# A graph layer on one core: ScalarE's copies ahead of its squares, a tail in another order, and an opening with gamma as a row

## The chip, the cores and the metric

The kernel runs on one core of a Trainium2 chip. The metric is the device time of one execution in microseconds (us), and less is better. The engines have instruction queues of their own: TensorE (PE in the profile, its weight loads PEld), VectorE (DVE), ScalarE (ACT), GpSimd (POOL) and SyncE (SP). An engine works through its queue in order; SP, ACT and POOL also start DMA transfers from theirs.

## The reference

A message-passing layer over 100,000 edges and 6,250 nodes of 128 features, then a residual sum and a layer norm:

```
msg_in = concatenate([x[src], x[dst], edge_attr])     # 100000 x 384
h   = msg_in @ W + b                                  # 100000 x 128
h   = (h - mean(h)) * rsqrt(var(h) + 1e-5) * gamma + beta
msg = relu(h)
out = segment_sum(msg, src, 6250)
return layernorm(x + out)                             # 6250 x 128
```

The edges come sorted by `dst`; `src` is in no order. All inputs are fp32 or int32.

## The kernel before, in words

*Folding.* W has three slices of 128 rows, for `x[src]`, `x[dst]` and the edge's own features. `weights` subtracts each row's mean and multiplies by the sign of gamma (`sgn`, from `signs`), so that the product has mean zero and only the sum of its squares is needed. `project` multiplies x by the first slice into an SBUF table `xa` (three bf16 parts that add up) and by the second into DRAM tables `xb_d`. TensorE does it in the first part of the run.

*Edges.* They lie in 782 tiles of 128, four tiles to a piece: 196 pieces, `q` in the code. For each piece

- SP loads the features (`eT`), the window of `xb_d` that holds the piece's destinations (`win`), and `db`, the destination's place in that window, spread over all partitions from a DRAM copy, `drel_d`. The pieces with `q < BY_PE` have no `db` load: TensorE spreads their row of `drel0` into PSUM with a product against ones. Piece 2's load is issued by POOL, all others by SP (L551).
- `edge_hot` (L577, VectorE) compares `db` with the partition number and so gives a one-hot `ohd`;
- `edges` (TensorE) adds the products `eT` x w (L589) and `ohd` x `win` (L593) in a PSUM tile `hp`;
- `evict` (ScalarE) copies `hp` (L601) and the source's number (L602) to one of eight buffers `hs`;
- `scatters` (L619, POOL) writes each tile with one indirect DMA to `sorted_d[s]`, at rows `place_i`: a bucket sort by source block. From piece 12 to 194 each scatter also waits for a named product of TensorE, so that it is spread over its piece.

`places` computes `place_i` on VectorE, for a group of tiles at a time, from the source numbers that `source_blocks` prepares. `first_windows` and `windows` cast the window places on ScalarE for the first pieces and for all. `clear` has SP fill the ends of the buckets from `empty`, a tile that `clean` fills by POOL's memsets.

*Pairs.* The edges are cut in six splits (`SPLITS`). When a split is sorted, its 50 source blocks are worked off in 25 pairs. A pair takes: a load of the sorted rows `hl`; `ones` (VectorE, a one-hot `ohe`, L691); `turn` (TensorE, its transposition, L703) and `turned` (ScalarE, a copy to `ohn`, L707); `seed` (ScalarE copies `hl` to a PSUM tile `sel`, L713); `pick` (TensorE adds the source's part of h from `xa`, L730); `square` (ScalarE, squares with their sums and the root, L739 and L742); `root` and `scale` (VectorE, L748 and L754: the reciprocal, and the scaled message with its cut at zero); `sums` (TensorE, L763) and `add` (VectorE, L771: into the table `acc`). A pair's tiles are in groups of at most four: two groups in the first four splits, a single one in the fifth.

`FLOW` is a list of these steps with an offset each; `work(n)` goes n steps forward and issues at each step what is due of the pairs under way, in the order of the list. A pair begins every four steps. `steps_due(q)` spreads the steps over the pieces; the fifth split's pairs stand in the last pieces, 1.56 pairs to a piece.

*Tail.* The sixth split's pairs are done in 14 `Unit`s behind the last scatter: one pair, eleven times two, one, one. A unit does what a pair does (load L792, `ones` L799, `turned` L812, `pick` L818 and L824, `square` L835 and L838, `scale` L850, `sums` L864, `add` L870) and then finishes its nodes: `begin` (POOL: `acc` times gamma's size, plus x, L882 and L883), `stats` (VectorE: plus beta's part, with row sums, L888), `var` (ScalarE: squares of the centred rows into `fsq`, their sums, and the root, L898 and L901), `norm` (VectorE, L907 and L909), `end` (POOL, two operations, L915 and L916; for the last unit ScalarE, L919) and the store to `out` (SP, L922). `tail(i)` writes down the order of step i, in which up to five units are at different places.

The order on TensorE, VectorE, ScalarE and SP is the order in which the program is written (`manual_schedule`); POOL's is left to the scheduler. Behind everything a flag is read on all engines (L1184), and a second, general path runs if it isn't zero (L1186); here it is zero.

Of the kernel before, what the change touches and what calls it, by code (L numbers as in the profile page):

```python
# [27 lines left out]
PT = 4  # L28
# [17 lines left out]
BY_PE = 2  # L46
# [37 lines left out]
def fast_path(ctx, tc, io, bad_d):  # L84
# [63 lines left out]
    nc.scalar.dma_start(gamma_bc, dram_ap(io["gamma"], 0, [[0, P], [1, D]]))  # L148
    nc.sync.dma_start(src_i[:, :n0], io["srcT"][:, :n0])
    nc.scalar.dma_start(w3[:, 1, :], w_in[:, 1, :])  # L150
    load_x(0, 1)
    nc.scalar.dma_start(dst0_i, io["dstC"][0:1, 0:BY_PE, :])
    nc.scalar.dma_start(base_i, io["base"])
    nc.scalar.dma_start(w3[:, 2, :], w_in[:, 2, :])
    nc.sync.dma_start(dst_i, io["dstC"])
# [3 lines left out]
    edge_feats(0)  # L159
# [6 lines left out]
    def late_loads():  # L166
        nc.scalar.dma_start(w3[:, 0, :], w_in[:, 0, :])
        for t, v in ((b_bc, io["b"]), (beta_bc, io["beta"])):
            nc.scalar.dma_start(t, dram_ap(v, 0, [[0, P], [1, D]]))
# [50 lines left out]

    def clean():
        for i in range(RUN):
            nc.gpsimd.memset(empty[:, i, 0:D], 0.0)
            nc.gpsimd.memset(empty[:, i, D:ROW], 0.0)
            nc.gpsimd.memset(empty[:, i, D:D + 1], 200.0)
# [17 lines left out]

    def signs():
        nc.vector.tensor_scalar(sgn, gamma_bc, 0.0, 2.0, op0=ALU.is_ge, op1=ALU.mult)
        nc.vector.tensor_scalar(sgn, sgn, -1.0, None, op0=ALU.add)
# [20 lines left out]
    def source_blocks(t0, t1):  # L267
        c = slice(t0, t1)
        nc.vector.tensor_copy(src_f[:, c], src_i[:, c])
# [5 lines left out]
        nc.vector.tensor_copy(bkt_h[:, c], bkt[:, c])  # L275

        nc.vector.tensor_scalar(src_f[:, c], bkt[:, c], 0.5, -0.25, op0=ALU.mult, op1=ALU.add)
        nc.vector.tensor_scalar(src_f[:, c], src_f[:, c], MAGIC, None, op0=ALU.add)
        nc.vector.tensor_scalar(src_f[:, c], src_f[:, c], -MAGIC, None, op0=ALU.add)
# [24 lines left out]
    def first_windows():  # L304
        nc.scalar.mul(minus00, dst0_i[:, :, 0], -1.0)
        for h in range(BY_PE):
            nc.scalar.activation(drel0[:, h, :], dst0_i[:, h, :], AF.Identity,
                                 bias=minus00[:, h:h + 1])
# [217 lines left out]

    def all_checks():
# [10 lines left out]
    clean()  # L538

    def edge_loads(q):  # L540
# [8 lines left out]
        if q >= BY_PE:  # L549
            c1 = g * PT * P  # L550
            (nc.sync if q > 2 else nc.gpsimd).dma_start(  # L551
# [228 lines left out]
    class Unit:  # L780
# [112 lines left out]
        def var(self):  # L893
            fin = late["fin"]
            fsq = fin.tile([P, D], F32, name="fsq", bufs=2)
            var = fin.tile([P, FN], F32, name="var", bufs=2)
            for j in range(self.m):
                nc.scalar.activation(fsq, self.y[:, j, :], AF.Square, scale=-float(D),  # L898
# [45 lines left out]

    constants()
    signs()
    weights(1, 2)
# [3 lines left out]
    first_windows()  # L951
    source_blocks(0, n0)
    run(groups[0])
    run(first)
    run(groups[0])
    bases([0])
    run(groups[0])
    run(first)
    run(groups[0], 2)
    windows()  # L960
    edge_loads(0)
    edge_loads(2)
    edge_window(0)
# [4 lines left out]
    weights(2, 3)  # L968
    run(first)
# [36 lines left out]
    others[at_slots[-1] + 4] = beta_row  # L1006

# [105 lines left out]
    def tail(i):  # L1113
# [51 lines left out]
    units[1].turn()  # L1165
    units[0].square()
    work(4)
# [10 lines left out]
def gnn_resnorm_kernel(ctx, tc, io):  # L1178
# [3 lines left out]
    with ExitStack() as inner:  # L1182
        fast_path(inner, tc, io, bad_t)
    flag = nc.values_load(bad_t[0:1, 0:1], min_val=0, max_val=1 << 20,  # L1184
                          skip_runtime_bounds_check_because="a sum of small counts")
    with tc.If(flag > 0):  # L1186
# [235 lines left out]
```

## Time and profile before

| | |
|---|---|
| time, median of three executions | 1142.15 us (1140.5 to 1145.27) |
| the profiled execution's own time | 1144.18 us |
| its span | 1142.4 us |
| TensorE | 77% busy, 8873 products |
| VectorE | 74%, 2352 instructions |
| ScalarE | 67%, 3115 instructions |
| POOL | 72%, 877 instructions, 782 of them scatters |
| HBM | 215 GB/s over the span |

The profile is a page with the busy time of each engine, the span in forty slices, the DMA queues, the chain of work that ended last, and the groups of instructions. A row of a group names line, engine, operation, output and inputs by the program's names, with the count; then the busy time, the mean of one in ns, the idle time ahead of them, and what ended most of it. Rows in order of time begin with the start and the duration in us, and end in brackets with the wait ahead of them and what ended it. Rows by stretch give the length, and then for an engine its busy time and count; in those for all engines the order is TensorE, its weight loads, VectorE, ScalarE, POOL, and then TensorE's granted clock, the DMA share and GB/s. Rows of waits give the engine, the tile, the line, the releaser, the sum, the count and the longest or mean wait in us.

### The profile page before, as it was taken

To read this page: it belongs to the slowest core of one execution; us is meant where nothing else is said; L and a number is where in the kernel's file an instruction comes from. 1 tells how busy PE (TensorE), PEld (TensorE's weight loads), DVE (VectorE), ACT (ScalarE), POOL (GpSimd) and SP (SyncE) were. 2 spreads that over 40 slices of the span, in tenths; PEclk is the share of its full clock that TensorE was granted. 3 is DMA by queue.
4 is the path that set the end of the run, shared out by engine and by line. 5 is a ranking of instruction groups with operands and counts; after the bars stand their busy time and mean duration, and the time that the engine had idled before them with its cause. 6 is when DMAs were issued, how large, how long until landed. Compare 5 with 4: busy or idle time off the path is not lost.

```text
span 1142.4 us, 27577 instructions
## 1 busy us (share of the span) xinstructions
PE 874.6 (77%) x8873; PEld 811.4 (71%) x8873; DVE 841.6 (74%) x2352; ACT 768.3 (67%) x3115; POOL 817.1 (72%) x877
## 2 busy tenths in 40 slices
PE   3668676537887869787787879888888998777993
PEld 2657565437787868787787869888887888775762
DVE  6875666236877777676868678987989887666984
ACT  3324432207676867677676778988889998776993
POOL 3677777777777777777777777777777776761675
PEclk9688887667988989899899989999999999999996
DMA  7698998457877763887786758776878676744531
GB/s 216 208 274 255 293 290 250 133 175 230 254 255 231 241 202 124 281 244 237 226 262 208 228 185 283 250 228 211 254 225 259 202 236 183 209 127 139 166 131 59
DMA packets 123539, 247.48 MB, mean 217 GB/s; under 512 B 47036, under 2 KB 55245, under 8 KB 123384
## 3 DMA queue, kind: packets, MB, share of 16 engines
q1 hardware_dynamic: 97332, 191.92, 55.0%
q0 software_dynamic: 25184, 53.31, 13.2%
q8 instruction: 71, 1.16, 0.4%
q14 instruction: 84, 0.69, 0.2%
q10 hardware_dynamic: 868, 0.40, 0.2%
HBM read 155.74 MB, written 89.80 MB: 215 GB/s over the span
## 4 chain that ended last, share of the span: by engine, by line
PE 31%; DVE 22%; DMA 22%; ACT 13%; issue 6%; POOL 4%; SPq 1%; ACTq 0%; POOLq 0%; DVEq 0%
DMA sorted<-hs,place_i 16%; PE pa L763 7%; PE sel L730 7%; PE hp L589 7%; DVE msg L754 5%; DMA db<-drel_d 4%; ACT sq L739 3%; DVE sc L437 3%; PE beside L484 3%; ACT sel L713 3%; DVE ohe L691 3%; ACT ohn L707 2%; POOL sorted L619 2%; ACT hs L601 2%; PE hp L593 2%
## 5 line engine op out<-in xcount | busy, mean ns | idle before, releaser
L619 POOL DMA_INDIRECT sorted<-hs,place_i x782 | 757.8, 969 | 253.6 <-issue 102.7
L730 PE MATMUL sel<-xa,ohn 128*128 128x128 bf16 x2550 | 188.1, 225 | 126.5 <-ACT sel L713 125.5
L730 PEld LDWEIGHTS <-ohn 128*128 128x128 bf16 x2550 | 165.4, 101 | 141.4 <-issue 111.4
L589 PE MATMUL hp<-w,eT 128*128 128x128 f32 x1564 | 241.5, 303 | 26.4 <-ACT hs L601 26.4
L739 ACT ACTIVATE sq<-sel 128x128 f32<-128x128 f32 x850 | 224.2, 281 | 47.4 <-PE sel L730 47.4
L589 PEld LDWEIGHTS hp<-w,eT 128*128 128x128 f32 x1564 | 218.8, 214 | 52.3 <-ACT hs L601 28.9
L754 DVE SCALAR_TENSOR_TENSOR msg<-sel,rstd,cut 128x128 f32<-128x128 f32 x850 | 240.7, 345 | 7.9
L601 ACT COPY hs<-hp 128x512 f32<-128x512 f32 x196 | 114.1, 582 | 195.3 <-DMA sorted<-hs,place_i 152.5
L763 PE MATMUL pa<-msg,ohe 128*128 128x130 f32 x1700 | 234.0, 291 | 3.5 <-DVE msg L754 3.0
L763 PEld LDWEIGHTS pa<-msg,ohe 128*128 128x128 f32 x1700 | 214.8, 203 | 5.3 <-DVE msg L754 4.3
L739 ACT ACTIVATION_READ_ACCUMULATOR sq<-sel 128x1 f32 x850 | 179.8, 212 | 0.0
L691 DVE TENSOR_TENSOR ohe<-hl,beside 128x1024 f32<-128x1024 f32 (+2 forms) x125 | 131.6, 1053 | 36.2 <-DMA hl<-sorted 24.5
L713 ACT COPY sel<-hl 128x512 f32<-128x512 f32 (+1 forms) x225 | 127.9, 568 | 14.4 <-DVE msg L754 14.1
L577 DVE TENSOR_SCALAR ohd<-db,part_w 128x512 bf16<-128x512 bf16 x194 | 72.1, 372 | 66.1 <-DMA db<-drel_d 41.3
L707 ACT COPY ohn<-tr 128x1024 bf16<-128x1024 bf16 (+2 forms) x125 | 108.7, 870 | 0.0
L748 DVE RECIPROCAL rstd<-std 128x4 f32<-128x4 f32 (+1 forms) x225 | 38.7, 172 | 91.1 <-ACT std L742 88.1
L593 PE MATMUL hp<-win,ohd 126*128 126x128 bf16 x782 | 82.9, 232 | 2.4 <-DMA win<-xb_d 2.4
L703 PE MATMUL tr<-ident_h,ohe 128*128 128x128 bf16 x850 | 70.4, 224 | 8.7 <-issue 7.4
L742 ACT ACTIVATE std<-ss,eps 128x4 f32<-128x4 f32 (+1 forms) x225 | 66.9, 297 | 7.3
L593 PEld LDWEIGHTS <-ohd 126*128 126x128 bf16 x782 | 66.7, 105 | 6.3 <-issue 2.6
L771 DVE TENSOR_TENSOR acc<-acc,pa 128x260 f32<-128x260 f32 x100 | 41.7, 417 | 29.4 <-PE pa L763 26.6
L703 PEld LDWEIGHTS <-ohe 128*128 128x128 bf16 x850 | 54.6, 100 | 9.4 <-issue 7.6
(193 smaller groups left out, 1038.6 us busy)
## 6 DMA issues: line engine op xcount, KB each, us to landing
eT<-in_eT SPq DMA_DIRECT2D x96, 512.0 KB
hl<-sorted SPq DMA_DIRECT2D x75, 528.0 KB
db<-drel_d SPq DMA_DIRECT2D x96, 256.0 KB
sorted<-empty SPq DMA_DIRECT2D x100, 198.0 KB
hl<-sorted SPq DMA_DIRECT2D x50, 264.0 KB
sorted<-hs,place_i POOLq DMA_INDIRECT x782
hl<-sorted SPq DMA_DIRECT2D x25, 396.0 KB
sorted<-empty SPq DMA_DIRECT2D x50, 132.0 KB
```

The source lines that it names most:

```text
L589: pe(nc.tensor.matmul(hp[:, j, :], eT[:, at], w[:, 2, :], start=j == 0, stop=False, skip_group_check=True), 4)
L593: pe(nc.tensor.matmul(hp[:, j, :], oh[:3 * WN, at], win[:3 * WN, :], start=False, stop=j == m - 1, skip_group_check=True))
L601: nc.scalar.copy(hs[:, :m, 0:D], hp[:, :m, :])
L619: i = nc.gpsimd.indirect_dma_start(out=sorted_d[s][:, :], out_offset=bass.IndirectOffsetOnAxis(ap=place_i[:parts, t:t + 1], axis=0), in_=h ...
L691: nc.vector.tensor_tensor(self.ohe[:, :k, :], self.hl[:, :k, D:D + 1].to_broadcast([P, k, P]), row_bc(iota_p, k), op=ALU.is_equal)
L703: pe(nc.tensor.transpose(tr[:, j, :], half[:, j0 + j, 1::2], ident_h))
L707: nc.scalar.copy(self.ohn[:, :self.k, :], self.tr[:, :self.k, :])
L713: nc.scalar.copy(self.sel[g][:, :m, :], self.hl[:, j0:j0 + m, 0:D])
L730: pe(nc.tensor.matmul(sel[:, j, :], self.ohn[:, j0 + j, :], xa[:, b, i * D:(i + 1) * D], start=False, stop=j == m - 1 and i == 2, skip_gro ...
L739: nc.scalar.activation(sq[:, j, :], self.sel[g][:, j, :], AF.Square, accum_out=ss[:, j:j + 1])
L754: nc.vector.scalar_tensor_tensor(self.msg[:, j0 + j, 0:D], self.sel[g][:, j, :], rstd[:, j:j + 1], cut, op0=ALU.mult, op1=ALU.max)
L763: pe(nc.tensor.matmul(self.pa[:, h, :], self.ohe[:, j, :], self.msg[:, j, :], start=(j == h), stop=(j == k - 2 + h)), 4)
```

## The change

There are four parts.

1. *The opening.* `BY_PE` goes from 2 to 4, so the first four pieces have no `db` load, and the load for piece 4 and all later ones is issued by SP. Gamma comes first as one row; VectorE makes its sign there, TensorE spreads it over the partitions with a product against ones, and ScalarE copies it to `sgn`. The broadcast load of gamma goes to the late loads. The opening's DMAs have another order. `clean` is done by ScalarE, with two copies from a small tile `none`. `source_blocks` and `first_windows` are in two halves, and ten products `warm_up` stand in TensorE's queue.
2. *Copies ahead of squares.* For pairs of a single group, `FLOW` issues `turned` and `seed` at offset 3 and `pick` at offset 5, in list order ahead of the square at 7; pairs of two groups keep their offsets.
3. *The tail.* `begin` of unit i-1 is issued ahead of `end` of unit i-3; `end` of the last two units is done by ScalarE, and `begin` of the last two by VectorE (before: the last one each). The squares in `var` go to slices of a `sq` tile in place of the two buffers `fsq`. The steps between the last pairs and the first units are interleaved in another order.
4. *The flag* is read in the middle of the run, right behind the step that computes it, and no longer at the end.

```
-BY_PE = 2
+BY_PE = 4
...
-    nc.scalar.dma_start(gamma_bc, dram_ap(io["gamma"], 0, [[0, P], [1, D]]))
-    nc.sync.dma_start(src_i[:, :n0], io["srcT"][:, :n0])
+    gamma_r = const.tile([1, D], F32, name="gamma_r")
     nc.scalar.dma_start(w3[:, 1, :], w_in[:, 1, :])
     load_x(0, 1)
-    nc.scalar.dma_start(dst0_i, io["dstC"][0:1, 0:BY_PE, :])
+    nc.scalar.dma_start(gamma_r, dram_ap(io["gamma"], 0, [[D, 1], [1, D]]))
+    nc.sync.dma_start(src_i[:, :n0], io["srcT"][:, :n0])
+    nc.scalar.dma_start(dst0_i, dram_ap(io["dstC"], 0, [[BY_PE * PT * P, 1], [PT * P, BY_PE],
+                                                        [1, PT * P]]))
     nc.scalar.dma_start(base_i, io["base"])
     nc.scalar.dma_start(w3[:, 2, :], w_in[:, 2, :])
+    edge_feats(0)
     nc.sync.dma_start(dst_i, io["dstC"])
     warm = const.tile([P, 1], F32, name="warm")
     nc.scalar.activation(warm, eps, AF.Sqrt)
-    edge_feats(0)
...
-        for t, v in ((b_bc, io["b"]), (beta_bc, io["beta"])):
+        for t, v in ((b_bc, io["b"]), (beta_bc, io["beta"]), (gamma_bc, io["gamma"])):
...
     def clean():
-        for i in range(RUN):
-            nc.gpsimd.memset(empty[:, i, 0:D], 0.0)
-            nc.gpsimd.memset(empty[:, i, D:ROW], 0.0)
-            nc.gpsimd.memset(empty[:, i, D:D + 1], 200.0)
+        nc.scalar.copy(flat(empty), none[:, 0:1].to_broadcast([P, RUN * ROW]))
+        nc.scalar.copy(empty[:, :, D], none[:, 1:2].to_broadcast([P, RUN]))
...
+    sgn_r = const.tile([1, D], BF16, name="sgn_r")
     def signs():
-        nc.vector.tensor_scalar(sgn, gamma_bc, 0.0, 2.0, op0=ALU.is_ge, op1=ALU.mult)
-        nc.vector.tensor_scalar(sgn, sgn, -1.0, None, op0=ALU.add)
+        nc.vector.tensor_scalar(gamma_r, gamma_r, 0.0, 2.0, op0=ALU.is_ge, op1=ALU.mult)
+        nc.vector.tensor_scalar(sgn_r, gamma_r, -1.0, None, op0=ALU.add)
+        spread = psum.tile([P, 512], F32, name="pa")[:, :D]
+        nc.tensor.matmul(spread, ones_h[0:1, :], sgn_r, start=True, stop=True)
+        nc.scalar.copy(sgn, spread)
...
+    def flags():
+        found.append(nc.values_load(
+            bad_d[0:1, 0:1], min_val=0, max_val=1 << 20,
+            skip_runtime_bounds_check_because="a sum of small counts"))
...
-            (nc.sync if q > 2 else nc.gpsimd).dma_start(
+            nc.sync.dma_start(
                 db[:, :c1], dram_ap(drel_d, t0 * P, [[0, P], [1, c1]]))
...
-            fsq = fin.tile([P, D], F32, name="fsq", bufs=2)
+            fsq = late["blk"].tile([P, PT, P], F32, name="sq")
...
-                nc.scalar.activation(fsq, self.y[:, j, :], AF.Square, scale=-float(D),
+                nc.scalar.activation(fsq[:, j, :], self.y[:, j, :], AF.Square, scale=-float(D),
...
+    def warm_up(n):
+        for _ in range(n):
+            ps = psum.tile([P, PT, P], F32, name="hp", bufs=2)
+            nc.tensor.matmul(flat(ps), ones_h, row_bc(ones_h, PT), start=True, stop=True)
+
+    warm_up(6)
     constants()
     signs()
+    warm_up(4)
+    source_blocks(0, n0, 0)
     weights(1, 2)
     groups = [project(0, 1)]
     run(groups[0])
     first, second = pieces[0][1], pieces[1][1]
-    first_windows()
-    source_blocks(0, n0)
-    run(groups[0])
-    run(first)
-    run(groups[0])
-    bases([0])
+    first_windows(0, 2)
+    source_blocks(0, n0, 1)
     run(groups[0])
     run(first)
     run(groups[0], 2)
+    run(first)
+    run(groups[0], 2)
+    weights(2, 3)
+    first_windows(2, BY_PE)
     windows()
+    clean()
     edge_loads(0)
     edge_loads(2)
+    run(first)
+    bases([0])
     edge_window(0)
     run(groups[0])
     for q in range(1, 3):
         edge_window(q)
     load_x(0, 0)
-    weights(2, 3)
-    run(first)
     edge_hot(0)
...
     others[at_slots[-1] + 4] = beta_row
+    others[at_slots[-1] + 5] = flags
...
+    def single(step):
+        return lambda x: step(x) if len(x.groups) == 1 else None
+
     FLOW = [(14, lambda x: x.add()), (11, second(lambda x: (x.root(1), x.scale(1)))),
             (9, lambda x: (x.root(0), x.scale(0))), (13, lambda x: x.sums()),
-            (8, second(lambda x: x.pick(1))), (6, lambda x: x.pick(0)),
-            (7, second(lambda x: x.seed(1))), (5, lambda x: x.seed(0)),
+            (8, second(lambda x: x.pick(1))), (6, second(lambda x: x.pick(0))),
+            (5, single(lambda x: x.pick(0))),
+            (7, second(lambda x: x.seed(1))), (5, second(lambda x: x.seed(0))),
+            (3, single(lambda x: (x.turned(), x.seed(0)))),
             (9, second(lambda x: x.square(1))), (7, lambda x: x.square(0)),
-            (4, lambda x: x.turned()), (2, lambda x: x.turn()),
+            (4, second(lambda x: x.turned())), (2, lambda x: x.turn()),
             (0, lambda x: x.ones()),
             (-6, None)]
...
         if at(i - 3):
             u(-3).norm()
-            u(-3).end(i - 3 == n - 1)
+            if i - 3 >= n - 2:
+                u(-3).end(True)
         if at(i - 1):
             for g in range(u(-1).n):
                 u(-1).add(g)
-            u(-1).begin(nc.vector if i == n else nc.gpsimd)
+            u(-1).begin(nc.vector if i >= n - 1 else nc.gpsimd)
+        if at(i - 3) and i - 3 < n - 2:
+            u(-3).end()
...
+    work(1)
+    units[0].ones()
+    units[3].load()
+    work(1)
+    units[0].turn()
+    work(1)
+    units[0].turned()
+    work(1)
+    units[0].pick(0)
+    units[0].xs_load()
+    units[1].ones()
     work(2)
-    units[3].load()
-    units[0].ones()
-    work(2)
-    units[0].turn()
-    units[0].turned()
-    work(3)
-    units[0].pick(0)
-    units[1].ones()
-    units[0].xs_load()
     units[1].turn()
     units[0].square()
-    work(4)
+    work(5)
...
-        fast_path(inner, tc, io, bad_t)
-    flag = nc.values_load(bad_t[0:1, 0:1], min_val=0, max_val=1 << 20,
-                          skip_runtime_bounds_check_because="a sum of small counts")
-    with tc.If(flag > 0):
+        found = []
+        fast_path(inner, tc, io, bad_t, found)
+    with tc.If(found[0] > 0):
```

More of the change, by code (lines that the diff above doesn't have):

```diff
@@ L81, in flat, with fast_path @@
     return t.rearrange("p t d -> p (t d)")
-def fast_path(ctx, tc, io, bad_d):
+def fast_path(ctx, tc, io, bad_d, found):
     nc = tc.nc
@@ L219, in fast_path @@
     empty = const.tile([P, RUN, ROW], F32, name="empty")
+    none = const.tile([P, 2], F32, name="none")
+    nc.vector.memset(none[:, 0:1], 0.0)
+    nc.vector.memset(none[:, 1:2], 200.0)
     def clean():
-        for i in range(RUN):
-            nc.gpsimd.memset(empty[:, i, 0:D], 0.0)
-            nc.gpsimd.memset(empty[:, i, D:ROW], 0.0)
-            nc.gpsimd.memset(empty[:, i, D:D + 1], 200.0)
+        nc.scalar.copy(flat(empty), none[:, 0:1].to_broadcast([P, RUN * ROW]))
+        nc.scalar.copy(empty[:, :, D], none[:, 1:2].to_broadcast([P, RUN]))
     def clear(s, p0, n, queue):
@@ L265, in fast_path, with source_blocks, source_rows @@
     src_f = setup.tile([P, TILES], F32, name="src_f")
-    def source_blocks(t0, t1):
+    def source_blocks(t0, t1, part=None):
         c = slice(t0, t1)
+        if part != 1:
+            source_rows(c)
+        if part != 0:
+            source_places(t0, t1, c)
+    def source_rows(c):
         nc.vector.tensor_copy(src_f[:, c], src_i[:, c])
@@ L275, in source_blocks, with source_places @@
         nc.vector.tensor_copy(bkt_h[:, c], bkt[:, c])
+    def source_places(t0, t1, c):
         nc.vector.tensor_scalar(src_f[:, c], bkt[:, c], 0.5, -0.25, op0=ALU.mult, op1=ALU.add)
@@ L302, in fast_path, with first_windows @@
     minus00 = setup.tile([1, BY_PE], F32, name="minus00")
-    def first_windows():
-        nc.scalar.mul(minus00, dst0_i[:, :, 0], -1.0)
-        for h in range(BY_PE):
+    def first_windows(h0, h1):
+        if h0 == 0:
+            nc.scalar.mul(minus00, dst0_i[:, :, 0], -1.0)
+        for h in range(h0, h1):
             nc.scalar.activation(drel0[:, h, :], dst0_i[:, h, :], AF.Identity,
@@ L537, in fast_path @@
         nc.gpsimd.memset(h[:, :, D:ROW], 0.0)
-    clean()
     def edge_loads(q):
```

## The prediction

> **What bounds the kernel now.** I read the page's group list first, then the scatters by stretch, then the instructions in order of time at the opening, at the last pairs and in the tail.
>
> ```profile
> L619 POOL DMA_INDIRECT sorted<-hs,place_i x782 | 757.8, 969 | 253.6 <-issue 102.7
> ```
>
> ```profile
> 52.70:700.00 647.30, 492.70 (x508) 0.86 0.74 232
> 951.40:1033.10 81.70, 55.98 (x58) 1.00 0.56 166
> 963.70:1033.10 69.40, 48.20 (x50) 1.00 0.54 159
> ```
>
> The second fence is the scatters alone by stretch (length, POOL busy, count). 508 of them take 647.3 us, 1.274 each, whatever the other engines do: POOL issues them without a break and paces the kernel. From 951.4 on one takes 1.41: there something else paces. ScalarE's waits confirm the long middle; it stands before full `hs` buffers:
>
> ```profile
> ACT hs L601 <- DMA sorted<-hs,place_i: 152.5, 57, 7.2
> ```
>
> So three parts can be shortened: the time until the scatters run without a break (52.7), the slow last stretch (951 to 1033), and the tail behind the last scatter.
>
> ```profile
> 18.30 0.74 DVE L577 TENSOR_SCALAR ohd<-sel,part_w 128x512 bf16<-128x512 f32 x1
> 19.09 0.59 ACT L601 COPY hs<-hp 128x512 f32<-128x512 f32 x1 [3.50 <-PE hp L593]
> 21.07 0.60 POOL L551 DMA_DIRECT2D db<-drel_d  x1 [4.38 <-DVE src_f L279]
> 21.99 1.03 POOL L619 DMA_INDIRECT sorted<-hs,place_i  x1 [0.31 <-issue]
> 26.11 0.35 DVE L577 TENSOR_SCALAR ohd<-db,part_w 128x512 bf16<-128x512 bf16 x1 [4.85 <-DMA db<-drel_d]
> 36.25 0.96 POOL L619 DMA_INDIRECT sorted<-hs,place_i  x1 [4.31 <-ACT hs L602]
> ```
>
> Opening: the first scatter is at 21.99 because a `db` load stands before it in POOL's queue. VectorE stands 4.85 us for the same load, and with it everything up to piece 2, so POOL is idle 4.31 us before 36.25.
>
> ```profile
> 1015.29 0.39 PE L703 MATMUL tr<-ident_h,ohe 128*128 128x128 bf16 x4
> 1015.55 0.28 ACT L739 ACTIVATE sq<-sel 128x128 f32<-128x128 f32 x1 [0.37 <-PE sel L730]
> 1016.93 0.57 ACT L707 COPY ohn<-tr 128x512 bf16<-128x512 bf16 x1
> 1017.06 0.18 DVE L748 RECIPROCAL rstd<-std 128x4 f32<-128x4 f32 x1 [1.14 <-ACT std L742]
> 1017.27 1.13 DVE L754 SCALAR_TENSOR_TENSOR msg<-sel,rstd,cut 128x128 f32<-128x128 f32 x4
> 1018.65 0.68 DVE L691 TENSOR_TENSOR ohe<-hl,beside 128x512 f32<-128x512 f32 x1
> 1018.97 0.28 ACT L739 ACTIVATE sq<-sel 128x128 f32<-128x128 f32 x1 [0.98 <-PE sel L730]
> ```
>
> Last pairs (one group of four): ScalarE goes round in 3.42 us (1015.55 to 1018.97): squares and root, two copies, then 0.98 idle until TensorE's products are there.
>
> ```profile
> 1081.00 0.35 DVE L888 SCALAR_TENSOR_TENSOR y<-beside,acc,y 128x128 f32<-128x128 f32 x1 [0.45 <-POOL y L883]
> 1082.35 1.04 POOL L915 TENSOR_TENSOR y<-y,frstd 128x512 f32<-128x512 f32 x1 [1.38 <-DVE frstd L907]
> 1084.46 1.18 POOL L882 TENSOR_TENSOR y<-acc,g 128x512 f32<-128x512 f32 x1
> 1087.02 0.35 DVE L888 SCALAR_TENSOR_TENSOR y<-beside,acc,y 128x128 f32<-128x128 f32 x1 [0.45 <-POOL y L883]
> 1066.00:1126.00 60.00, 53.07 (x468) 40.06 (x465) 50.83 (x217) 52.58 (x260) 44.36 (x41) 0.97 0.39 132
> ```
>
> Tail: a two-pair unit takes 6.02 us (1081.00 to 1087.02), round a ring: VectorE's `stats` and `norm` (1.35, to 1082.35), POOL's `end` (2.11, to 1084.46), POOL's `begin` (2.56), `stats` again. VectorE idles only 0.45 of it, so it needs 5.57. The last row is the busy time in ten units (TensorE, its weight loads, VectorE, ScalarE, POOL): TensorE 5.3 and ScalarE 5.3 a unit.
>
> **The change, part by part.** The sum is made against the profiled run, 1144.18 us with a span of 1142.4; the median of the three runs is 1142.15, 2.0 less, so I take the saving from that.
>
> *Opening.* With `BY_PE` at 4, TensorE spreads the windows of pieces 2 and 3, and POOL's `db` load is gone. POOL could start some 0.3 of issue behind `hs` of piece 0 (19.09 and two copies, 0.7): near 20.1; its first eight scatters then last to 30.4. VectorE's 4.85 wait goes, and it reads two pieces from PSUM at 0.74 instead of 0.35: what follows moves by 4.1 to 4.9; I take 4.5. Upper bound 5.5 (some row work earlier besides). Lower bound, the lead that pieces fed by later loads already have over POOL:
>
> ```profile
> 55.17 0.20 ACT L602 COPY hs<-sloc 128x4 f32<-128x4 f32 x1
> 57.82 0.97 POOL L619 DMA_INDIRECT sorted<-hs,place_i  x1 [0.30 <-issue]
> ```
>
> If piece 6 comes no sooner, the stream gains 57.82 less 55.37, 2.45. What is late next is VectorE's own work for piece 5.
>
> Added on ScalarE: two casts more, a PSUM copy of the sign, two copies that clear `empty`, one late DMA issue.
>
> ```profile
> 5.76 1.28 ACT L158 ACT_TABLE_LOAD   x1 [5.76 <-DMA gamma_bc<-in_gamma]
> 7.38 1.33 ACT L307 ACTIVATE drel<-dst_i,minus 1x512 bf16<-1x512 int32 x2
> 7.43 0.35 DVE L252 SCALAR_TENSOR_TENSOR w<-w,wmean,sgn 128x128 f32<-128x128 f32 x1
> 12.95 1.05 ACT L311 CAST dst_f<-dst_i 98x1024 f32<-98x1024 int32 x1
> ```
>
> Two casts are 1.33, clearing about 1.1 (the row at 12.95 is nearest in size) and 0.2, the issue 0.4: 3.0 in all, under the 3.50 that ScalarE waits before `hs` of piece 0. Without that cover piece 0 is 3.0 late, and POOL has its eight done 2 after piece 2 is there. The sign now takes TensorE and then ScalarE, whose queue first stands for a DMA lane until W's slice has landed (near 5.4, as `gamma_bc` did in that place), issues twice (0.7), loads its table (1.28) and copies (0.28): near 7.75, against `w` at 7.43 now. From 1 early to 1 late; VectorE's row work that moves ahead of it makes up for 0.3, so zero. The warm-up products run while TensorE waits for weights, and I count on no faster clock: zero. POOL's memsets fell in time in which it had nothing to do: zero. On SP the `db` load of piece 4 stands as before, with a window load and clears behind it: zero with the leads above.
>
> *Last pairs.* ScalarE copies for pair p+1 before it squares pair p, so TensorE's products run under squares. ScalarE's own work is 3.42 less the idle 0.98, 2.44. A second bound is a ring: from the root of p (ScalarE free at 1016.93) the reciprocal starts 0.13 later, then 0.21, scaling and addition 1.38, `ohe` of p+3 0.68, transposition 0.45: the copy of p+3 can begin 2.85 later; with ScalarE's 2.44 for it, two pairs take 5.29, 2.65 each. A piece has 1.56 pairs: 4.13, an eviction 0.6 and some 0.3 where a piece's products stand before a transposition: 5.0, just under four scatters, 5.1. So POOL paces again: 50 x 1.274 = 63.7 instead of 69.4, 5.7 won. The flag is now read in mid-stream, 0.5 on each engine (SP's row of now):
>
> ```profile
> L1184 SPq TENSOR_LOAD <-bad_t x1: 492/492/492, 1134.9 to 1134.9; - x1
> ```
>
> Net 5.2. Upper bound 7.8 (from 951.4: 81.7 less 73.9); lower bound zero, the round staying at 3.42.
>
> *Start of the tail.* The last scatter ends at 1033.1.
>
> ```profile
> 1035.83 4.05 SPq L792 DMA_DIRECT2D hl<-sorted  x5
> 670.95 4.17 DMA hl<-sorted
> 1046.55 1.22 DVE L799 TENSOR_TENSOR ohe<-hl,beside 128x1024 f32<-128x1024 f32 x1
> 1048.48 1.01 ACT L812 COPY ohn<-tr 128x1024 bf16<-128x1024 bf16 x1 [0.41 <-PE tr L809]
> ```
>
> Unit 0's load goes out 2.7 later, when that scatter has landed; but unit 1's `ohe` begins 13.5 later, behind five pairs of 3.42. At 2.65 these are done 4 sooner, and the load is what is late: 2.7, a landing of some 3.7 (4.17 in the chain of waits for twice the bytes), `ohe` of unit 0 0.7, pair 23 1.3, an addition 0.3: unit 1's `ohe` near 8.7. Its `ohn` follows the squares of pair 24 and of unit 0, near 10.9 instead of 15.4. Gain 4.5; 1 if loads take twice as long, 6 if the squares don't hold it up.
>
> *Units.* `begin` goes ahead of `end` on POOL. The ring is then `stats` and `norm` 1.4, two additions 0.7, `begin` 2.56: 4.7. The separate slices for the variance squares take work off ScalarE, which was no bound. VectorE's 5.57 is: I take 5.62 for seven units, then 5.5, 5.3 and 4.75 as VectorE has less `ohe` to make: 54.9 instead of 60.2. Gain 5.3; bounds 0, and 12.7 if the ring alone held. What `begin`'s wait for the additions holds up: `end` of an older unit, its store, and behind that on SP the next `xs` and `hl` loads, about 2.5 later and needed a period after they land: zero, once 2.5 if not.
>
> *Last units.* Unit 12's `begin` moves to VectorE, ahead of unit 13's scaling, while POOL runs `end` of unit 10.
>
> ```profile
> 1121.85 1.26 POOL L883 TENSOR_TENSOR y<-y,xs 128x512 f32<-128x512 f32 x1
> 1128.91 1.04 POOL L915 TENSOR_TENSOR y<-y,frstd 128x512 f32<-128x512 f32 x1 [0.83 <-DVE frstd L907]
> 1129.40 0.83 DVE L882 TENSOR_TENSOR y<-acc,g 128x256 f32<-128x256 f32 x1
> 1130.27 1.15 DVE L883 TENSOR_TENSOR y<-y,xs 128x256 f32<-128x256 f32 x1
> 1133.62 0.88 ACT L919 ACTIVATE y<-y,shift,frstd 128x128 f32<-128x128 f32 x2 [0.43 <-DVE shift L909]
> ```
>
> Beside POOL's `end`, VectorE's `begin` takes 2.0, in which it scales nothing. From the last two-pair `begin` to the end it is now 11.4 (1123.1 to 1134.5); I make it 11.9 with that 2.0 in the chain. 0.5 lost, from 2 lost to 1 won. The Trainium skill, SBUF — State Buffer, Who interferes with whom, says that a VectorE instruction with two SBUF inputs and a POOL instruction that reads SBUF lock each other out for the whole instruction, which speaks against this move. The trace agrees: the 0.83 ends 0.28 behind POOL's 1.04. Without such a lock I would put `begin` at 0.7, and the sum at 20.5. At the very end SP's flag read goes, partly beside the store: 0.3.
>
> Sum: 4.5 + 5.2 + 4.5 + 5.3 - 0.5 + 0.3 = 19.3; 1142.15 - 19.3 = 1122.8 us.
>
> **The rivals.**
> 1. *The units stay at 6.0*: VectorE, TensorE and ScalarE are each over 5.2 busy and hold each other up. For it, how little play there is; against it, none but VectorE waits on POOL. 5.3 lost: 1128; with the opening at its lower bound, 1130.
> 2. *VectorE's 5.57 shrinks* too, since some of it is time shared with POOL, and the ring's 4.7 decides: 12.7 instead of 5.3, 1115. Against it, most of VectorE's operations here read PSUM.
> 3. *The copies win nothing*: the copy for p+1 needs a transposition that stands behind the products of p. For it, that order; against it, products (0.98) and transposition (0.39) just fit under squares and root (1.38). 5.2 and 4 of the tail's start lost: 1132. With rival 1 besides, 1137, no measurable change.
> 4. *Slower*: the same order closes the ring through VectorE tighter. If `ohe` of p+3 comes one pair later, each pair takes the whole 5.29: 25 pairs add 47, 10 is won elsewhere, 1179. It decides once VectorE runs over 2.65 behind; against it, VectorE idles 1.14 a pair now.
>
> **How the numbers follow.** Forecast 0.59, with its own range 1117 to 1128 (opening, pairs and tail each some us off); rival 1 0.16, rival 2 0.08, rival 3 0.05, no measurable change 0.04, slower 0.08. A measurement of this kernel tells 0.5%, 5.7 us, from no change. 1114 to 1133 takes in the forecast and rivals 1 to 3. Faster 0.88, same 0.04, slower 0.08.
>
> **What would show it.** Right: the first scatter near 20 and no 4 us of idle before piece 2; 1.27 per scatter to the end, the last near 1023; copies ahead of squares with no wait between; units at 5.6 with `end` behind `begin`. Wrong: a `db` or `hl` wait in place of those removed, scatters still at 1.4 after 950, units at 6.0, ScalarE idle before `ohn` in the last pairs.

## The result, and the profile after

The changed kernel takes 1133.76 us (median of four, 1130.05 to 1135.62), the kernel before 1142.24 beside it: a ratio of 0.9908, with a 95% interval of 0.988 to 0.9936. That is 8.5 us won, less than half of the 19.3 forecast, and 0.8 above the upper end of the range. A second measurement (the reference run below) gives 1133.49 against 1143.1, 0.9923 (0.9901 to 0.9944). The ratios are those of the record and not the quotients of these medians, which are 0.9926 and 0.9916.

The page's group lines for the sums of the pairs in the kernel before, and for the scatters and the same sums in the changed kernel:

```profile
L763 PE MATMUL pa<-msg,ohe 128*128 128x130 f32 x1700 | 234.0, 291 | 3.5 <-DVE msg L754 3.0
L640 POOL DMA_INDIRECT sorted<-hs,place_i x782 | 759.0, 971 | 247.3 <-issue 99.6
L784 PE MATMUL pa<-msg,ohe 128*128 128x130 f32 x1700 | 233.6, 291 | 19.5 <-DVE acc L792 16.1
```

The scatters alone in the long middle (length, POOL busy, count, clock, DMA share, GB/s):

```profile
52.70:700.00 647.30, 492.49 (x508) 0.87 0.74 232
```

The middle is untouched: again 508 scatters in 647.3 us. The sums have a wait that was not there, 16.1 us for the addition that empties `pa`; before, their whole idle time was 3.5.

To see where the time went, I cut the span at the same events in each trace: the start of the 101st and of the 701st scatter, the end of the last, the first instruction of `stats` of the first and of the twelfth unit, the end of ScalarE's last instruction, the end. The last two columns are experiments told of below.

```
stretch, us                       before   after  after again  old flow  old opening
start to 101st scatter            155.18  148.01     149.24     148.86     151.46
101st to 701st scatter            764.16  764.62     764.37     763.68     765.53
701st to end of last scatter      113.75  108.59     109.71     114.16     109.12
last scatter to first stats        24.62   21.31      21.32      23.04      21.90
first stats to twelfth unit's      65.44   65.46      65.43      65.43      65.43
... to end of ScalarE's last       11.34   13.10      13.09      13.09      13.09
... to the end                      7.90    7.17       7.31       7.13       7.31
span                             1142.39 1128.26    1130.47    1135.39    1133.84
```

The opening, the last pairs and the start of the tail are shorter; the units in the tail take exactly what they took; the last units take 1.75 more. The opening differs by microseconds between executions of the same code: before's 155.18 is 3.7 above the old opening's other trace. The two profiled executions differ by 14.1 us and the medians by 8.5, since before's stands 1.9 above its median and the changed kernel's 3.7 below.

The opening of the changed kernel, in order of time:

```profile
5.83 0.35 DVE L261 SCALAR_TENSOR_TENSOR w<-w,wmean,sgn 128x128 f32<-128x128 f32 x1
17.83 1.04 POOL L640 DMA_INDIRECT sorted<-hs,place_i  x1 [2.88 <-DVE sloc L286]
29.85 0.97 POOL L640 DMA_INDIRECT sorted<-hs,place_i  x1 [2.05 <-ACT hs L623]
```

`w` is there at 5.83 instead of 7.43, the first scatter at 17.83 instead of 21.99, and the gap ahead of piece 2 is 2.05 instead of 4.31.

The last pairs, behind the last scatter, in order of time:

```profile
1021.59 0.30 ACT L763 ACTIVATE std<-ss,eps 128x4 f32<-128x4 f32 x1
1022.13 1.13 DVE L775 SCALAR_TENSOR_TENSOR msg<-sel,rstd,cut 128x128 f32<-128x128 f32 x4
1022.99 0.59 ACT L728 COPY ohn<-tr 128x512 bf16<-128x512 bf16 x1 [1.11 <-PE tr L724]
1023.17 0.41 DVE L792 TENSOR_TENSOR acc<-acc,pa 128x260 f32<-128x260 f32 x1
1023.64 1.16 PE L784 MATMUL pa<-msg,ohe 128*128 128x130 f32 x8 [0.69 <-DVE acc L792]
1024.64 0.83 PE L751 MATMUL sel<-xa,ohn 128*128 128x128 bf16 x12
1025.31 0.39 PE L724 MATMUL tr<-ident_h,ohe 128*128 128x128 bf16 x4
1025.73 0.59 ACT L728 COPY ohn<-tr 128x512 bf16<-128x512 bf16 x1 [0.25 <-PE tr L724]
1027.91 0.30 ACT L763 ACTIVATE std<-ss,eps 128x4 f32<-128x4 f32 x1
```

This is the new ring, two pairs long: root at 1021.59, message, addition, then the sums that wait for it, behind them on TensorE the products and the transposition, the copies, the squares, and the root at 1027.91. 6.32 for two pairs, 3.16 each; before it was 3.42.

A two-pair unit in the tail:

```profile
1071.85 0.35 DVE L909 SCALAR_TENSOR_TENSOR y<-beside,acc,y 128x128 f32<-128x128 f32 x1 [0.47 <-POOL y L904]
1073.19 1.04 POOL L936 TENSOR_TENSOR y<-y,frstd 128x512 f32<-128x512 f32 x1 [1.38 <-DVE frstd L928]
1074.31 1.04 POOL L937 TENSOR_TENSOR y<-y,shift 128x512 f32<-128x512 f32 x1
1075.31 1.19 POOL L903 TENSOR_TENSOR y<-acc,g 128x512 f32<-128x512 f32 x1
1076.58 1.27 POOL L904 TENSOR_TENSOR y<-y,xs 128x512 f32<-128x512 f32 x1
1077.88 0.35 DVE L909 SCALAR_TENSOR_TENSOR y<-beside,acc,y 128x128 f32<-128x128 f32 x1 [0.47 <-POOL y L904]
```

L936 and L937 are `end`, L903 and L904 are `begin`. On POOL `end` still stands ahead of `begin`, though the program is now written the other way round, and the period is 6.03. The fourth part of the change stopped at the same queue: four engines read the flag between 930 and 937, but POOL's read stands at 1114.9, in the tail (before: 1132.9).

The last two units:

```profile
1110.46 1.10 POOL L937 TENSOR_TENSOR y<-y,shift 128x512 f32<-128x512 f32 x1
1110.69 1.15 DVE L904 TENSOR_TENSOR y<-y,xs 128x256 f32<-128x256 f32 x1
1114.91 1.04 POOL L937 TENSOR_TENSOR y<-y,shift 128x512 f32<-128x512 f32 x1
1115.05 1.19 DVE L903 TENSOR_TENSOR y<-acc,g 128x256 f32<-128x256 f32 x1
1116.27 0.42 DVE L904 TENSOR_TENSOR y<-y,xs 128x256 f32<-128x256 f32 x1
1116.73 0.35 DVE L909 SCALAR_TENSOR_TENSOR y<-beside,acc,y 128x128 f32<-128x128 f32 x1
1117.66 0.88 ACT L940 ACTIVATE y<-y,shift,frstd 128x128 f32<-128x128 f32 x2 [3.07 <-DVE shift L930]
1118.45 0.38 ACT L919 ACTIVATE sq<-y,total 128x128 f32<-128x128 f32 x1
```

ScalarE's `end` of unit 12 (L940) is issued ahead of the variance squares of unit 13 (L919), and waits until 1117.66 for unit 12's `norm`; the squares could have begun behind the first `stats` instruction, near 1117.1.

### The profile page after: what moved, and what is told of

The parts are those of the page before. It is cut to its first block, busy times and chain, and to the rows that moved or that the text cites. A ratio compares the mean times of both kernels' runs of the same rounds, so it can differ in the third digit from the quotient of the medians.

```text
span 1128.3 us, 27527 instructions
## 1 busy us (share of the span) xinstructions
PE 877.3 (78%) x8886; PEld 809.8 (72%) x8886; DVE 840.7 (75%) x2356; ACT 768.6 (68%) x3122; POOL 813.4 (72%) x848
## 3 DMA queue, kind: packets, MB, share of 16 engines
q8 instruction: 71, 1.16, 0.4%
## 4 chain that ended last, share of the span: by engine, by line
PE 34%; DMA 21%; DVE 20%; ACT 13%; issue 6%; POOL 3%; SPq 1%; ACTq 0%; POOLq 0%; DVEq 0%
DMA sorted<-hs,place_i 16%; PE pa L784 9%; PE hp L610 9%; PE sel L751 7%; DVE msg L775 5%; PE beside L501 4%; ACT sq L760 3%; DMA db<-drel_d 3%; ACT sel L734 3%; DVE sc L454 3%; ACT hs L622 2%; DVE ohe L712 2%; PE hp L614 2%; PE tr L724 2%; POOL sorted L640 1%
## 5 line engine op out<-in xcount | busy, mean ns | idle before, releaser
L622 ACT COPY hs<-hp 128x512 f32<-128x512 f32 x196 | 114.0, 582 | 200.2 <-DMA sorted<-hs,place_i 153.4
L784 PE MATMUL pa<-msg,ohe 128*128 128x130 f32 x1700 | 233.6, 291 | 19.5 <-DVE acc L792 16.1
```

Source lines behind the costliest of these rows:

```text
L622: nc.scalar.copy(hs[:, :m, 0:D], hp[:, :m, :])
L784: pe(nc.tensor.matmul(self.pa[:, h, :], self.ohe[:, j, :], self.msg[:, j, :], start=(j == h), stop=(j == k - 2 + h)), 4)
```

## The experiments

The theory after the result: the opening, the copies, the start of the tail and the exit came about, but in the units POOL kept its order because its queue alone is not written by hand, and the last units lose by ScalarE's new `end`. The rivals: the units are held at 6.0 by VectorE, TensorE and ScalarE whatever POOL does; the gain is not from the places that the forecast named.

**POOL's order in the tail.**

```
-            engine.tensor_tensor(self.y, acc[:, b0:b0 + m, 0:D], row_bc(g2, m), op=ALU.mult)
+            keep(engine.tensor_tensor(self.y, acc[:, b0:b0 + m, 0:D], row_bc(g2, m), op=ALU.mult))
...
```

The same stands around the other operation of `begin` and the two of `end`; `keep` pins an instruction of POOL behind the one written before it.

> The changed kernel with one thing added: POOL's two operations of begin and of end are kept in the order in which the program is written, so that begin really stands ahead of end. The forecast's own reasoning expects 5.6 us from one two-pair unit to the next instead of the 6.03 that the changed kernel shows, about 60 us instead of 65.5 from the first unit's stats to the twelfth's, and a span about 5 us shorter. Rival 1 (VectorE, TensorE and ScalarE hold each other up) expects 6.0 and the same span within 1 us. Rival 2 (VectorE needs less once POOL stands elsewhere) expects 4.7 and 12 us.

This run and the next three fell on a chip on which the kernel before takes 1388.1 us, 21% more (the last section shows what differs there); the ratio here is 0.9944 (0.9922 to 0.9965). In the stretch of the units that chip shows the changed kernel's 6.03 too, so the units can be compared. A period of `pool_order` in order of time (L904 and L905 are its `begin`, L938 and L939 its `end`):

```profile
1317.97 1.04 POOL L938 TENSOR_TENSOR y<-y,frstd 128x512 f32<-128x512 f32 x1
1318.74 0.34 DVE L910 SCALAR_TENSOR_TENSOR y<-beside,acc,y 128x128 f32<-128x128 f32 x1
1319.09 1.04 POOL L939 TENSOR_TENSOR y<-y,shift 128x512 f32<-128x512 f32 x1
1320.95 1.19 POOL L904 TENSOR_TENSOR y<-acc,g 128x512 f32<-128x512 f32 x1 [0.82 <-DVE acc L891]
1322.22 1.28 POOL L905 TENSOR_TENSOR y<-y,xs 128x512 f32<-128x512 f32 x1
1324.22 0.34 DVE L910 SCALAR_TENSOR_TENSOR y<-beside,acc,y 128x128 f32<-128x128 f32 x1
```

The busy time over four units, in the order TensorE, its weight loads, VectorE, ScalarE, POOL:

```profile
1307.80:1329.69 21.89, 21.89 (x213) 17.33 (x212) 21.61 (x89) 21.17 (x111) 18.00 (x17) 1.00 0.58 185
```

With `begin` truly ahead, a unit takes 5.48, `stats` waits for POOL no more, and VectorE is busy 21.61 of 21.89. TensorE is shown busy all the time, but so it is in the changed kernel's longer units (24.04 of 24.11), so that its share tells nothing here; ScalarE's 21.17 is not far below VectorE, but the last run below gives it more work and a unit takes no longer. So VectorE is what is left; no run takes work off it to show that. From the first stats to the twelfth unit's it is 59.65 instead of 65.46: 5.8 won. The forecast's 5.62 a unit was near for an order that the change does not bring about; rivals 1 and 2 fall.

**Unit 12's end back on POOL.**

```
-            if i - 3 >= n - 2:
+            if i - 3 >= n - 1:
...
-        if at(i - 3) and i - 3 < n - 2:
+        if at(i - 3) and i - 3 < n - 1:
```

> The changed kernel with the end of unit 12 back on POOL; its begin stays on VectorE. The theory that ScalarE's end of unit 12 (two operations, 0.88 us) stands ahead of unit 13's variance squares expects these to begin right behind the first stats of unit 13, and 1.2 us less from unit 13's stats to the end of ScalarE's last operation (4.4 us in the changed kernel). The rival, that the loss in the last units is VectorE's begin of unit 12 alone, expects no difference there.

The first `stats` of unit 13, its first variance square and ScalarE's last operations, in order of time, in `end_pool`:

```profile
1364.92 0.35 DVE L909 SCALAR_TENSOR_TENSOR y<-beside,acc,y 128x128 f32<-128x128 f32 x1
1365.32 0.40 ACT L919 ACTIVATE sq<-y,total 128x128 f32<-128x128 f32 x1 [2.53 <-DVE y L909]
1367.10 0.88 ACT L940 ACTIVATE y<-y,shift,frstd 128x128 f32<-128x128 f32 x2 [0.57 <-DVE shift L930]
```

The squares begin 0.40 behind `stats` instead of 1.72, and from that `stats` to ScalarE's end it is 3.05 instead of 4.36. The stretch of the last units is 11.78 here, 13.09 and 13.10 in the next two runs, which keep it on ScalarE on the same chip. This is a single execution (1377.29 us), read by its stretches alone. So 1.3 of the 1.75 lost in the last units is that `end` on ScalarE; the theory holds.

**The old opening and the old list of steps, twice.** In the one, every line of the opening is before's again; in the other, only this:

```
-            (5, single(lambda x: x.pick(0))),
-            (3, single(lambda x: (x.turned(), x.seed(0)))),
...
+            (8, second(lambda x: x.pick(1))), (6, lambda x: x.pick(0)),
+            (7, second(lambda x: x.seed(1))), (5, lambda x: x.seed(0)),
...
+            (4, lambda x: x.turned()), (2, lambda x: x.turn()),
```

> The changed kernel with the whole opening of before (two pieces by TensorE, piece 2's load on POOL, gamma loaded to all partitions, the old order, no warm-up products); pairs, tail and flag as changed. If the lead of 7.2 us that the scatters have in the middle of the run is carried to the end: the last scatter and the span 7 us later. If it is lost where the other engines set the pace (from piece 150 on): 0 to 2 us later.

> The changed kernel with the list of pair steps of before (copies behind squares), all else as changed. The theory that the copies ahead of the squares give the last pairs their pace expects the rounds of single-group pairs at 3.4 us again, 4.7 to 5.2 us on the last scatter, and 2 to 4 more until the second unit's one-hot: a span 7 to 9 us longer. The rival, that the copies win nothing and the lead comes from the rest, expects no more than 1 us.

On that first chip the ratios are 0.9996 (0.9976 to 1.0016) and 0.9947 (0.9926 to 0.9968). They settle nothing: the scatters do not pace that chip's middle, the changed kernel itself was not among these four runs, and so both were run again on a chip on which the kernel before takes 1143.1, beside the changed kernel.

> The changed kernel once more, as the reference for the three beside it on the same chip, and for how much its stages move between executions. If the difference of 14.1 us between the two profiled executions is the change's own: a ratio of 0.988 to 0.990. If the 8.4 us of the medians is: 0.992 to 0.994.

> The old opening with the new pairs and tail again. If the lead in the middle of the run is carried to the end: first scatter 4.2 us later, the hundredth 7.2 us, last scatter and span 7 us later than the changed kernel. If the engines at the end set the pace by themselves: no more than 2 us later at the last scatter.

> The old list of pair steps again. The theory that the copies ahead of the squares set the pace of the last pairs expects 4.7 to 5.2 us later at the last scatter and 2 to 4 more until the second unit's one-hot, 7 to 9 us on the span. The rival expects no more than 1 us. Beside the pieces the gaps between scatters of more than 1.6 us come back (11 before, 6 in the changed kernel).

The changed kernel takes 1133.49 there, with the old opening 1137.45 (0.9952, 0.9936 to 0.9968), with the old list 1138.57 (0.9964, 0.9954 to 0.9975). So the opening is worth 4.0 by the medians, about half of the 7 expected; in the table above its 101st scatter is 2.2 to 3.5 later than with the new opening, and the lead is still 2.8 to 4.9 at the last scatter (1026.11 against 1023.32 and 1021.22): it is carried through. The list of steps is worth 5.1 by the medians, below the 7 to 9 expected: 4.5 to 5.6 between the 701st and the last scatter, as expected, and 1.7 up to the first stats instead of 2 to 4. Of the 3.3 won at the start of the tail, 1.6 is there with the old list too (23.04 against 24.62): with the list as before, what is left for it is the run-up's new order.

**Two pieces by load.**

```
-BY_PE = 4
+BY_PE = 2
```

> The changed kernel with BY_PE back at 2, so pieces 2 and 3 take the load of db, which SP issues; the rest of the opening as changed. The forecast's reasoning, that this load holds piece 2 up, expects the ninth scatter 2.5 to 4 us later (30.0 to 30.8 in four executions with BY_PE at 4, 33.3 with the old opening), and the span 2 to 4 us longer. The rival, that the window loads set piece 2's start anyway, expects 0 to 1.

SP's first loads for the pieces, in order of time:

```profile
16.84 0.33 SPq L572 DMA_DIRECT2D db<-drel_d  x1
18.00 0.92 SPq L584 DMA_DIRECT2D win<-xb_d  x1
```

SP stands for `drel_d` before it issues the load of `db` at 16.84, and the first window load behind it goes out at 18.00 instead of 13.02. The first scatter moves to 23.27, the ninth to 33.52, as late as was expected, and the stream has no gap from there; the 101st is at 151.18. That is as late as with the old opening (151.46), where six executions with `BY_PE` at 4 have it between 147.36 and 149.81. The time is 1133.83, 0.9927 (0.991 to 0.9945): beside 1133.49 and 1133.76, on other chips, no difference that these runs can tell, where 2 to 4 was expected. On the same chip stands only the next run, the changed kernel without its warm-up products, at 1132.06; its four executions all lie below these four, by 1.8 in the medians. So the traces speak for the spread by TensorE as what the opening wins by, with some 2 us, but the time against the changed kernel does not show it.

**No warm-up products.**

```
-    warm_up(6)
...
-    warm_up(4)
```

> The changed kernel without the ten products that stand ahead in TensorE's queue. In two of four executions of the new opening the first projection took 1.16 us for eight products, in two 2.08, as without them before. If the products help at all by the clock: 2.08 always, and the first scatter 0 to 0.9 us later on the mean (19.0 over four executions). The forecast said zero, and the span the same within 1 us.

1132.06, 0.9916 (0.9899 to 0.9933). The first projection took 2.08 and the first scatter came at 20.00, later than in the six executions with the products, but the 101st at 148.92 is among theirs, and nothing was lost by the time: zero, as forecast.

**A better version.** POOL in program order, unit 12's `begin` and `end` both on POOL, and for pairs of one group

```
-    FLOW = [(14, lambda x: x.add()), (11, second(lambda x: (x.root(1), x.scale(1)))),
-            (9, lambda x: (x.root(0), x.scale(0))), (13, lambda x: x.sums()),
+    FLOW = [(14, second(lambda x: x.add())), (13, single(lambda x: x.add())),
+            (11, second(lambda x: (x.root(1), x.scale(1)))),
+            (9, lambda x: (x.root(0), x.scale(0))), (13, second(lambda x: x.sums())),
...
             (4, second(lambda x: x.turned())), (2, lambda x: x.turn()),
+            (10, single(lambda x: x.sums())),
```

> The changed kernel with POOL kept in program order in the tail, unit 12's begin and end both on POOL, and for pairs of one group the sums issued behind the transposition and the addition ahead of the next root, so that no pick stands behind a sum that waits for an addition. Expected from the rows: 5.8 us less in the units (5.47 each instead of 6.03), 1.3 from unit 13's stats to the end, some 1 us less from VectorE's begin of unit 12, and with rounds of 2.6 us instead of 3.16 in the pairs behind the last scatter 0 to 2.5 us there: 8 to 10 us less than the changed kernel. The rival, that the pairs' rounds are set by ScalarE and TensorE together and not by the addition, expects 3.16 still and 7 to 8 us in all.

1124.98, 0.9846 (0.9823 to 0.9869): 8.5 below the changed kernel, 18.1 below the kernel before. The copies in the last pairs:

```profile
1024.04 0.59 ACT L728 COPY ohn<-tr 128x512 bf16<-128x512 bf16 x1 [0.30 <-PE tr L724]
1026.77 0.59 ACT L728 COPY ohn<-tr 128x512 bf16<-128x512 bf16 x1 [0.25 <-PE tr L724]
1028.91 0.69 DVE L820 TENSOR_TENSOR ohe<-hl,beside 128x512 f32<-128x512 f32 x1 [1.01 <-DMA hl<-sorted]
```

A round is 2.73: the addition was in the ring, and the rival (3.16 still) falls. What is late next is the load of unit 0, for which VectorE now waits 1.01. From the last scatter to the first stats it is 18.61 instead of 21.3, but from the 701st to the last scatter 111.16, some 2 more. The two together are 129.8, and 129.9 and 131.0 in the changed kernel's two traces: the shorter rounds win next to nothing. The gain is in the tail, 59.66 for the units, now on a chip like the first one, and 10.66 instead of 13.10 behind them, with 0.8 given back at the very end (8.03), which I did not follow up. The next version moves the sums only in the pairs that run behind the last piece, by a mark that is set there:

```
+    def total(x, free=False):
+        if not hasattr(x, "pa") and (late.get("free") or not free):
+            x.sums()
...
+            (10, single(lambda x: total(x, True))),
...
+    late["free"] = True
     work(n_tail - n_steps)
```

> As the best version so far (POOL in program order in the tail, unit 12's begin and end on POOL), but the sums go behind the transposition only in the pairs that run after the last piece; beside the pieces the changed kernel's order stays. If the 2 us that the earlier version lost between the 700th and the last scatter (111.2 against 108.6 to 109.7) come from pieces whose products stand behind sums that wait for a scaled message: about 109 again, 18.6 from the last scatter to the first stats, and a span 1.5 to 2 us below the earlier version (1122 to 1124 by the median). If not: 111 again, and no difference.

0.9842 (0.9823 to 0.9861), no different from the version before it. The 109 came back (109.83), but the start of the tail is 20.42 and not 18.6: together 130.3 again. The scatters end sooner and the first unit's stats do not. The last part is the variance squares:

```
-            fsq = late["blk"].tile([P, PT, P], F32, name="sq")
+            fsq = fin.tile([P, D], F32, name="fsq", bufs=2)
```

> The version before, with the variance squares written to the two alternating tiles of before in place of slices. In the trace of before such a square follows the last after 0.52 us, in the changed kernel after 0.39, four in a unit: 0.5 us of ScalarE. If the slices matter only once POOL's order is mended: units of 5.8 to 6.0 us instead of 5.47. If ScalarE has room: 5.47 still.

The single execution took 1121.82, and its units stay at 5.47 with squares every 0.53 us. ScalarE has room for that, and the separate slices are worth nothing that the units show, in the changed kernel or in this one.

## Why the prediction failed in size

Faster was right, and so were most of the places; the sum was too big by 10.8 us, about half of it one step, the units.

*Opening, 4.5: about right.* 4.0 by the medians. The time does not show that it is won by the spread of the pieces 2 and 3, as the forecast has it; the start of the 101st scatter in `by_pe_2` speaks for it. The sign was taken for no gain, with `w` near 7.75; it was there at 5.83, since ScalarE's queue stood only until 3.41 and not until 5.4. The first scatter was forecast near 20.1; it came between 17.83 and 19.65 in six executions of the new opening. But the working had a fault: the profiled execution of before stood 2.0 above its median, and its opening is long (155.18 at the 101st scatter; 151.46 in the other execution of the same opening, which in turn stood 1.8 below its median). I took every stretch for typical and subtracted from the median.

*Last pairs, 5.2 net: right in size, wrong in the way.* 4.0 to 5.2 between the 701st and the last scatter. POOL paces again, as forecast: the last 50 scatters take 64.5 (forecast 63.7). But the round is 3.16, not 2.65: the sum "two pairs take 5.29" left out that a transposition stands on TensorE behind sums that wait for the addition and behind the products, 1.0 and 0.67 more, less the 0.68 of the one-hot that is not in that ring. That the size came out was partly luck: beside the pieces two rounds take 6.3 as well (3.01 and 3.31, for instance), so the eviction, which the sum put on top, fits into the ring's waits, and 1.56 rounds are 4.9, still under four scatters. The flag's 0.5 is not seen where it is read, at 930 to 937 on four engines: scatters there follow each other by 1.27. The gaps behind it (2.09 and 2.58, before 1.93 and 2.30) are not told apart from it.

*Start of the tail, 4.5: 3.3.* The second unit's one-hot came 8.6 behind the last scatter, forecast 8.7; its copy 11.3, forecast 10.9. The rest went behind them: unit 1's squares stood 2.23 for products behind the last pair's sums.

*Units, 5.3: nothing.* The step that failed is its first sentence, "`begin` goes ahead of `end` on POOL". Of all queues only POOL's is left to the scheduler, as the text said of the kernel before, and on POOL the changed kernel has `end` ahead of `begin` as before: 65.43 to 65.46 over the units, where before has 65.44. The forecast named "units at 6.0" as a sign of being wrong, and this is what came. That the change doesn't do what it says was not among the rivals, where it belonged. With the order forced, 5.8 is won. The rivals' 1128 to 1132 were nearer in number, and for reasons that fell: the units were not held at 6.0 by the other engines, and the copies did win.

*Last units, 0.5 lost: 1.75 lost.* `begin` on VectorE beside POOL's `end` took the 2.0 forecast (1109.82 to 1111.84). What was not priced at all is the other moved step, unit 12's `end` on ScalarE: 1.3. (The 20.5 that the forecast gives for a `begin` of 0.7 would be 20.6.) The rule of the Trainium skill (SBUF — State Buffer, Who interferes with whom), that a VectorE instruction with two SBUF inputs and a POOL instruction that reads SBUF lock each other out, is borne out again: the 1.19 of L903 ends 0.29 behind POOL's operation, and L904 of the same size takes 0.42 once POOL is idle.

*Exit, 0.3: 0.6 to 0.7* (7.90 to 7.17 and 7.31).

Measured, that is 4.0 + 4.6 + 3.3 + 0 - 1.75 + 0.65 = 10.8, against 8.5 and 9.6 in the two comparisons, whose intervals reach from 7.3 to 13.7 and from 6.4 to 11.3. Why before's opening is long in one execution and short in another is not settled: the loads land at other times (the second slice of W was worked on at 10.09 in one execution of the changed kernel and at 11.67 in the other), but no run here made them late on purpose.

## What to carry to other kernels

An edit of program order is an edit only on queues that follow program order; look at the built queue of the engine it is meant for before costing it. When a wait is removed from a ring, write the next ring down as a list of every queue that it passes, with what stands ahead on each; here a sum waiting for an addition held the products behind it. And a single profiled execution that stands above its median has its excess somewhere: find the stretch before working out a saving in it.

## What the runs showed of the hardware

One chip ran the kernel before in 1388.1 us. There TensorE pauses between products and waits for nothing that the profile shows (TensorE alone, in the run `end_pool`):

```profile
636.17 0.33 PE L784 MATMUL pa<-msg,ohe 128*128 128x130 f32 x1
637.53 0.40 PE L784 MATMUL pa<-msg,ohe 128*128 128x130 f32 x2 [1.03 <-issue]
638.98 0.36 PE L784 MATMUL pa<-msg,ohe 128*128 128x130 f32 x1 [1.05 <-issue]
640.39 2.96 PE L784 MATMUL pa<-msg,ohe 128*128 128x130 f32 x12 [1.05 <-issue]
```

In this stretch it is one or two products, then 1.05 us of nothing. Over the span such pauses of TensorE add up to 204 us there, 240 of them, and to 7.8 us, two of them, in the changed kernel's own trace. The 600 scatters from the 101st on take 954.5 us instead of 764.6, and ScalarE's waits for scatters to land fall from 153.4 us to 25.6. So POOL, which is the pace of the middle elsewhere, often waits for others there, and a change's worth is another one. What makes the pauses no run shows.

Ten products ahead do not settle how fast the first projection runs: its eight products took 1.16 us in six executions with them and 2.08 in four (`after_again` and `best_all` are one of each), and 2.08 in all four without. The profile's granted clock reads 1.00 over these products in both kinds, so it does not tell them apart.

In `pool_order` an instruction of VectorE with two small inputs in SBUF (`shift`, 128x4) took 0.80 instead of 0.16 where it began 0.26 behind an operation of POOL, and ended with it (in four units 0.63 to 0.80):

```profile
1346.35 1.04 POOL L939 TENSOR_TENSOR y<-y,shift 128x512 f32<-128x512 f32 x1
1346.61 0.80 DVE L931 SCALAR_TENSOR_TENSOR shift<-total,frstd 128x4 f32<-128x4 f32 x1
```
